# Attention 1 of a graph kernel: the scatter in bfloat16 with three-part messages, the dense sums with the operands exchanged

## The chip, the cores and the metric

The kernel runs on one core of a Trainium2 chip. The metric is the device time of one execution in microseconds (us). A core has five engines with queues of their own, each strictly in order: PE (matrix products), DVE (vector), ACT (scalar functions and copies), POOL (here the issuer of gathers) and SP (the issuer of most DMAs).[...]

## The reference

Two graph layers over 6,250 nodes and 200,000 edges sorted by destination. The first is two graph attentions, the second a convolution with an MLP over edge attributes. The change touches the first attention (4 heads of 16 features):

```python
feat = (x @ W).reshape(num_nodes, H, D)
el = jnp.sum(feat * attn_l[None], axis=-1)
er = jnp.sum(feat * attn_r[None], axis=-1)
e = jax.nn.leaky_relu(el[src] + er[dst], NEG_SLOPE)
m = jax.ops.segment_max(e, dst, num_segments=num_nodes)
ee = jnp.exp(e - m[dst])
s = jax.ops.segment_sum(ee, dst, num_segments=num_nodes)
alpha = ee / s[dst]
msg = feat[src] * alpha[:, :, None]
rst = jax.ops.segment_sum(msg, dst, num_segments=num_nodes)
```

## The kernel before

Nodes are cut into 49 blocks of 128 destinations. Attention 1 treats them in two ways, mixed in one stretch of time.

**Blocks 0 to 30, by edges.** For each block up to 34 chunks of 128 edges are gathered (POOL, L315, one indirect DMA per chunk) in five groups, four of eight chunks and one of two. `attend` (L353) makes for each group a one-hot matrix of destinations on DVE (`one_hot`, L324: `ohr`, four bytes per element), fetches the destination's factors with a matmul per chunk (L360), multiplies them into the gathered features (`msg`, L364 to L370), and splits the message into two parts of the format fp32r, the rounded value by a cast on ACT (L331) and the rest by a subtraction on DVE (L332). Its `scatter` sums with one matmul per chunk: the one-hot is the stationary operand, the two parts side by side (136 columns) are the moving one (L377). When a block is done, ACT copies the first half of the sums and DVE adds the second (L967, L968).

**Blocks 31 to 48, by counts.** For a pair of blocks and each of 7 groups of 7 source blocks, `dense1` (L830) takes a table of how many edges lead from a source node to a destination (`ctc`). For each of four heads ACT makes seven ramps of 128 x 256 (L870), DVE takes the minimum of ramps and counts (`up`, L872, bf16), and PE sums the sources' features over it (L890): the minima of one block are the stationary operand, 102 columns of `rc` (two exponentials x 17 features x three bf16 parts) the moving one, so 14 matmuls for seven source blocks and two destination blocks. Once per group of seven, PE also sums over the plain counts (`every`, L884), here already with the features stationary and 256 columns of counts moving. In `end` (L895) ACT copies `every` to SBUF, PE transposes it, and DVE reduces, subtracts and weighs; the sums of L890 stand with destinations as rows already. `rc` is read from a table `rhs1` in DRAM that `fill_rhs1` (L667) writes in seven steps while blocks 1 and 2 run.

Beside both, `count` (L743) builds the count tables: DVE makes the pair-wise one-hots `lo` and `key` from `slots` (L752, bf16, in PSUM), PE multiplies them (L763), ACT casts the result (L765, `ca`) and issues its DMA to DRAM.

The order is the program's, refined by the scheduler of the tile framework. A hand-written loop gives each group of `attend` a share of counting steps and dense steps. A step's matmuls are put off to the step after it:

```python
    def step(new):

        while late:
            late.popleft()()
        late.extend(new)
```

After attention 1 come attention 2 (all blocks by counts, L1165 to L1170) and the convolution (L1212 on, with `one_hot` and the two-part split of L331 and L332 again).

Of the kernel before, what the change touches and what calls it, by code (L numbers as in the profile page):

```python
# [42 lines left out]
P = 128  # L43
# [23 lines left out]
def gnn_kernel(ctx: ExitStack, tc: tile.TileContext, x, src, dst, attr4, attr8,  # L67
# [207 lines left out]
    srcw = pool.tile([P, NB, K], I32, name="srcw")  # L275
    dstw = pool.tile([P, NB, K], F32, name="dstw")
    raw_dst = {}
# [40 lines left out]

    def one_hot(dl, n, exact=True):
        if exact:  # L320
            oh = work.tile([P, SB, P], F32R, name="ohr", bufs=3)
        else:
            oh = gen.tile([P, GSB, P], F32, name="ohg")
        nc.vector.tensor_tensor(oh[:, :n, :], slot[:, None, :].to_broadcast([P, n, P]),  # L324
                                dl[:, :, None].to_broadcast([P, n, P]), op=OP.is_equal)
        return oh

# [25 lines left out]
    def attend(G, dl, n, oht, pq, H, acc_of, start, stop):  # L353

        oh = one_hot(dl, n)
        pe = ps_pe.tile([P, 512], F32, tag="pe", name="pe")
        for c in range(n):
            nc.tensor.matmul(pe[:, c * 6 * H:(c + 1) * 6 * H], oht[:, c, :], pq, start=True, stop=True)  # L360
        w = aw.tile([P, SB, 2 * H], F32, name=f"w{H}")
        nc.vector.tensor_reduce(w[:, :n, :], pe[:, :n * 6 * H].rearrange("p (c j s) -> p c j s", c=n, s=3),
                                axis=AX.X, op=OP.add)
        nc.vector.tensor_tensor(w[:, :n, :], w[:, :n, :], G[:, :n, HD + H:], op=OP.mult)  # L364
        m = aw.tile([P, SB, HD + H], F32, name=f"msg{H}")
        nc.vector.tensor_tensor(m[:, :n, HD:], w[:, :n, :H], w[:, :n, H:], op=OP.max)
        nc.vector.tensor_tensor(
            m[:, :n, :HD].rearrange("p c (h d) -> p c h d", h=H),
            G[:, :n, :HD].rearrange("p c (h d) -> p c h d", h=H),
            m[:, :n, HD:][:, :, :, None].to_broadcast([P, n, H, HD // H]), op=OP.mult)  # L370
        ms = aw.tile([P, SB, 2, HD + H], F32R, name="halves")
        halve([ms[:, :n, j, :] for j in range(2)], m[:, :n, :])

        def scatter():
            acc = acc_of()
            for c in range(n):
                nc.tensor.matmul(acc, oh[:, c, :], ms[:, c].rearrange("e s f -> e (s f)"),  # L377
                                 start=start and c == 0, stop=stop and c == n - 1)

        return scatter  # L380

    def attend_general(G, dl, n, erc, H, acc, start, stop):


        oh = one_hot(dl, n, False)
        pt = quad()
# [22 lines left out]
    def node_max(G, dl, n, H, most):  # L409

        oh = one_hot(dl, n, False)
        for c in range(n):
# [249 lines left out]
    C1 = 3 * (DH + 1)  # L662
    W1R = 2 * H1 * C1 + 2
    rhs1 = dram.tile([P, NB, W1R], BF16, name="rhs1")
    deg1 = pool.tile([P, DENSE1], F32, name="deg1")

    def fill_rhs1(b0, n):  # L667
        t = dn.tile([P, HS, R1], F32, name="t1c", bufs=1)
        nc.sync.dma_start(t[:, :n], rows_of(table1, b0, n))
        x = dn.tile([P, HS, 2, H1, DH + 1], F32, name="x1", bufs=1)  # L670
        for j in range(2):
            ex = t[:, :n, HD + (1 + j) * H1:HD + (2 + j) * H1]
            nc.vector.tensor_tensor(x[:, :n, j, :, :DH], t[:, :n, :HD].rearrange("p b (h d) -> p b h d", h=H1),
                                    ex[:, :, :, None].to_broadcast([P, n, H1, DH]), op=OP.mult)
            nc.vector.tensor_copy(x[:, :n, j, :, DH:], ex[:, :, :, None])
        r = dn.tile([P, HS, W1R], BF16, name="rc")
        nc.vector.memset(r[:, :, 2 * H1 * C1:], 1.0)
        for j in range(2):
            rj = r[:, :, j * H1 * C1:(j + 1) * H1 * C1].rearrange("p b (f s) -> p b f s", s=3)
            xj = x[:, :n, j].rearrange("p b h d -> p b (h d)")  # L680
            nc.scalar.copy(rj[..., 0], xj)
            nc.vector.tensor_tensor(xj, xj, rj[..., 0], op=OP.subtract)
            nc.scalar.copy(rj[..., 1], xj)
            nc.vector.tensor_tensor(rj[..., 2], xj, rj[..., 1], op=OP.subtract)
        nc.sync.dma_start(rhs1[:, b0:b0 + n], r)
# [144 lines left out]
    def dense1():  # L830
# [14 lines left out]
        for b0 in range(NG, NB, 2):  # L845
# [3 lines left out]
            for h in range(0, H1, 2):  # L849
# [6 lines left out]
                nc.scalar.copy(erb[:, h:h + 2, :n * P], pe.rearrange("p (j c) -> p j c", j=2)[:, :, :n * P])  # L856

            sums = {}
            yield []
            for h0 in range(0, NB, HS):  # L860
                ct, r = ahead
                if h0 + HS < NB:
                    ahead = load(b0, n, h0 + HS)
                by_head = r[:, :, :2 * H1 * C1].rearrange("p b (j h f) -> p b j h f", j=2, h=H1)
                for h in range(H1):
# [9 lines left out]

                    def add(h0=h0, h=h, r=r, ct=ct, up=up, by_head=by_head, b0=b0, n=n, sums=sums):
                        if h0 + h == 0:
                            sums["ups"] = [ps_dn.tile([P, 512], F32, tag=f"up{k}", name=f"up{k}")[:, :2 * H1 * C1].rearrange(
                                "p (h j f) -> p h j f", h=H1, j=2) for k in range(n)]
                            sums["every"] = ps_dn.tile([P, 2, 2 * P], F32, tag="every", name="every")  # L880
                        ups, every = sums["ups"], sums["every"]
                        for i in range(HS if h == 0 else 0):
                            for j in range(2):
                                nc.tensor.matmul(every[:HH + 1, j, :n * P].rearrange("p (k d) -> p k d", d=QN),  # L884
                                                 r[:, i, (2 + j) * HH:(3 + j) * HH + 1],
                                                 ct[:, :n, :, i, :].rearrange("p k a d -> p (k a) d"),
                                                 start=h0 + i + j == 0, stop=h0 + i + j == NB)
                        for i in range(HS):
                            for k in range(n):
                                nc.tensor.matmul(ups[k][:, h], up[:, i, k * P:(k + 1) * P], by_head[:, i, :, h, :],  # L890
                                                 start=h0 + i + h == 0, stop=h0 + i + h == NB + H1 - 2)

                    yield [add]

            def end(b0=b0, n=n, sums=sums):  # L895
# [4 lines left out]
                for k in range(n):  # L900
                    for j in range(2):
                        nc.tensor.transpose(turned[:, k, j, :HH + 1], whole[:, j, k * P:(k + 1) * P],
                                            ident[:HH + 1, :HH + 1])
                s2 = dn.tile([P, 2, H1, DH + 1], F32, name="s2", bufs=1)
                v = dn.tile([P, 2, 2, H1, DH + 1], F32, name="v1", bufs=1)
                for k in range(n):
                    nc.vector.tensor_reduce(s2[:, k].rearrange("p (j h) d -> p j (h d)", j=2),
                                            turned[:, k, :, :HH].rearrange("p j (f s) -> p j f s", s=3),
                                            axis=AX.X, op=OP.add)
                    for j in range(2):  # L910
                        nc.vector.tensor_reduce(v[:, k, j], ups[k][:, :, j].rearrange("p h (d s) -> p h d s", s=3),
                                                axis=AX.X, op=OP.add)
                nc.vector.tensor_copy(deg1[:, b0 - NG:b0 - NG + n, None], turned[:, :n, 1, HH:HH + 1])
                nc.vector.tensor_tensor(v[:, :n, 1], s2[:, :n], v[:, :n, 1], op=OP.subtract)
                for j in range(2):
                    nc.vector.tensor_tensor(v[:, :n, j], v[:, :n, j],
                                            pq[:, b0:b0 + n, j * H1:(j + 1) * H1, None].to_broadcast([P, n, H1, DH + 1]),
                                            op=OP.mult)
                total = fin.tile([P, 2, HD + H1], F32, name="sumsd")
                nc.vector.tensor_add(total[:, :n, :HD].rearrange("p k (h d) -> p k h d", h=H1), v[:, :n, 0, :, :DH],  # L920
                                     v[:, :n, 1, :, :DH])
                nc.vector.tensor_add(total[:, :n, HD:, None], v[:, :n, 0, :, DH:], v[:, :n, 1, :, DH:])
                finish1(b0, n, total[:, :n, :])
# [30 lines left out]
    def attending(b, s, n, oht):  # L954
# [3 lines left out]
        def acc_of():  # L958
            if s == 0:
                kept1["acc"] = whole()[:, :2 * (HD + H1)]  # L960
            return kept1["acc"]

        def end():
            if b % 4 == 0:
                kept1["sums"] = fin.tile([P, 4, HD + H1], F32, name="sums1", bufs=2)
            acc, sums = kept1["acc"], kept1["sums"]
            nc.scalar.copy(sums[:, b % 4, :], acc[:, :HD + H1])  # L967
            nc.vector.tensor_add(sums[:, b % 4, :], sums[:, b % 4, :], acc[:, HD + H1:])  # L968
            if b % 4 == 3 or b == NG - 1:
# [316 lines left out]
    with tc.tile_pool(name="conv", bufs=1) as pool, tc.tile_pool(name="gath3", bufs=6) as gath:  # L1286
# [10 lines left out]
        def hots(t):  # L1297
            n = min(SB, NT - t)
            return one_hot(dstc[:, t:t + n], n)

# [55 lines left out]
        def general3(b, n):  # L1356
            nc.vector.tensor_copy(base, starts[:, ds(b, 1)])
            nc.vector.memset(tot3, 0.0)
            with tc.For_i(0, NCHUNK, 1) as i:
# [11 lines left out]
                for s in range(0, GK, GSB):  # L1371
# [4 lines left out]
                    for c in range(GSB):  # L1376
# [3 lines left out]
                    convolve(G, GSB, at[0][:, cs, 0:1], at[0][:, cs, 1:], a8t,  # L1380
                             lambda c: (acc, s + c == 0, s + c == GK - 1), one_hot(dl[:, cs], GSB))
                for j in range(2):
# [47 lines left out]
```

## Time and profile before

| | |
|---|---|
| median of 3 runs | 4651.73 us (4643.12 to 4654.26) |
| the profiled execution, its span | 4651.0 us, 4649.3 us |
| busy, share of span | DVE 75%, PE 69%, ACT 61%, POOL 60%, PE weight loads 51% |
| granted PE clock, mean | 0.754 |
| moved by DMA | 480.88 MB, 103 GB/s |

Busy shares are means over three stages with different limits, so the stage in question must be read by itself. In the rows of the groups the order is: line, engine, operation, what is written and read, shapes and count; then after the bar the busy time in us, the mean of one in ns; then the engine's idle time just before the group and what ended most of it. Rows of waits give who waited for whom, us in total, how often, and the longest. PE's busy time overlaps itself, because matmuls are pipelined.

### The profile page before, as it was taken

Reading aid. Unit: us, or ns where it says so; the run is one execution under the profiler, and the core shown is the slowest. Engines: PE = TensorE matmul, PEld = TensorE weight load, DVE = VectorE, ACT = ScalarE, POOL = GpSimd, SP = SyncE. Lnnn points to the kernel's source line nnn. Section 1 sums busy time; section 2 is a strip of 40 time slices with the busy share of each in tenths; the row PEclk is TensorE's granted clock in tenths of the full one; section 3 lists DMA queues with packets and bytes.
Section 4 is the critical chain, followed back from the end, with each engine's and each line's share of the span. In section 5 each row is a group of like instructions: output and inputs, shape, how many; then the busy total and the mean of one; then the engine's idle time right before and its main releaser. Section 6 shows DMA issues by size and latency. Waiting matters only on the chain. (4 is left out here: it accounts for less than half of the span.)

```text
span 4649.3 us, 65503 instructions
## 1 busy us (share of the span) xinstructions
PE 3221.1 (69%) x21547; PEld 2384.9 (51%) x21548; DVE 3499.3 (75%) x5685; ACT 2828.8 (61%) x6834; POOL 2785.6 (60%) x2684
## 2 busy tenths in 40 slices
PE   3023676766667766399997678777777777777777
PEld 3013566656566666388885344444444444444444
DVE  4255777878778878488886787788878777878787
ACT  2022578777878888499996554555555555555554
POOL 0677777666566665100002777777777777777774
PEclk9999766666666666599998676677677777766777
DMA  3344455555555555544442222222222222222221
GB/s 86 69 108 125 139 162 145 157 151 156 144 150 163 164 152 149 184 159 157 160 165 73 57 58 59 58 58 58 58 57 59 58 58 58 58 58 58 58 57 32
DMA packets 348162, 480.88 MB, mean 103 GB/s; under 512 B 190737, under 2 KB 236343, under 8 KB 343830
## 3 DMA queue, kind: packets, MB, share of 16 engines
q1 hardware_dynamic: 199542, 240.46, 16.9%
q0 software_dynamic: 85776, 147.31, 13.4%
q10 hardware_dynamic: 62480, 88.68, 5.6%
q8 instruction: 176, 2.88, 0.3%
q14 instruction: 188, 1.54, 0.1%
HBM read 367.21 MB, written 108.97 MB: 102 GB/s over the span
## 5 line engine op out<-in xcount | busy, mean ns | idle before, releaser
L315 POOL DMA_INDIRECT G<-table,srcc x1563 | 1592.8, 1019 | 1027.5 <-DVE kept L1210 551.4
L315 POOL DMA_INDIRECT G<-table,srcw x1054 | 1121.0, 1064 | 568.2 <-issue 279.0
L1262 PE MATMUL whole<-halves,ohr 128*128 128x512 f32 x1563 | 684.8, 596 | 362.2 <-DVE halves L332 320.1
L870 ACT ACTIVATE ramp<-erb,sel 128x256 bf16<-128x256 f32 x1764 | 759.0, 499 | 11.5 <-DVE up L872 8.0
L1262 PEld LDWEIGHTS whole<-halves,ohr 128*128 128x128 f32 x1563 | 427.5, 288 | 607.6 <-DVE halves L332 392.5
L1243 ACT ACTIVATE g<-G,a 128x128 f32<-128x128 f32 x1563 | 511.0, 395 | 43.5 <-DMA G<-table,srcc 35.0
L1161 ACT ACTIVATE ramp<-small,sel 128x256 bf16<-128x256 f32 (+1 forms) x1225 | 447.6, 625 | 61.1 <-DVE up L1165 26.1
L765 ACT CAST ca<-small 128x392 bf16<-128x392 f32 x784 | 342.1, 481 | 192.1 <-PE small L763 180.4
L890 PE MATMUL up<-rc,up 128*128 128x102 bf16 x3528 | 311.4, 264 | 155.9 <-DVE up L872 154.8
L377 PE MATMUL whole<-halves,ohr 128*128 128x136 f32 x1054 | 250.1, 387 | 224.6 <-DVE halves L332 167.7
L763 PE MATMUL small<-key,lo 128*128 128x98 bf16 x3136 | 318.6, 252 | 116.1 <-ACT ca L765 105.3
L1232 PEld LDWEIGHTS big<-wtp_sb,hid 64*128 64x128 f32 x3126 | 256.7, 239 | 204.7 <-ACT hid L1226 100.7
L890 PEld LDWEIGHTS <-up 128*128 128x128 bf16 x3528 | 265.7, 129 | 183.4 <-DVE up L872 177.4
L332 DVE TENSOR_TENSOR halves<-big,halves 128x1024 fp32r<-128x1024 f32 x196 | 237.4, 1211 | 144.3 <-ACT halves L331 144.3
L872 DVE TENSOR_TENSOR up<-ramp,ctc 128x1792 bf16<-128x1792 bf16 x252 | 273.9, 1087 | 92.7 <-ACT ramp L870 71.3
L1224 PE MATMUL small<-hid,wm_sb 128*128 128x512 f32 x392 | 288.0, 825 | 74.4 <-ACT hid L1222 74.2
L377 PEld LDWEIGHTS whole<-halves,ohr 128*128 128x128 f32 x1054 | 217.3, 292 | 237.1 <-DVE halves L332 172.4
L1232 PE MATMUL big<-wtp_sb,hid 64*128 64x128 f32 x3126 | 307.4, 344 | 26.8 <-ACT hid L1226 26.8
L763 PEld LDWEIGHTS <-lo 128*128 128x128 bf16 x3136 | 247.1, 124 | 145.1 <-issue 126.4
L752 DVE TENSOR_TENSOR lo<-slots,turned 128x2048 bf16<-128x2048 bf16 x196 | 239.0, 1219 | 101.4 <-PE small L763 100.2
L1222 ACT ACTIVATE hid<-small 128x512 f32<-128x512 f32 x196 | 116.8, 596 | 313.7 <-PE small L1220 313.7
L331 ACT CAST halves<-mid 128x1024 fp32r<-128x1024 f32 x196 | 204.1, 1041 | 160.9 <-DVE mid L1251 159.2
(292 smaller groups left out, 6196.7 us busy)
## 6 DMA issues: line engine op xcount, KB each, us to landing
counts<-ca ACTq DMA_DIRECT2D x196, 392.0 KB
ct<-counts SPq DMA_DIRECT2D x196, 392.0 KB
rc<-rhs SPq DMA_DIRECT2D x63, 717.5 KB
oht<-dlow SPq DMA_DIRECT2D x31, 1088.0 KB
ctc<-counts SPq DMA_DIRECT2D x504, 56.0 KB
G<-table,srcc POOLq DMA_INDIRECT x1563
G<-table,srcw POOLq DMA_INDIRECT x1054
a8t<-attr_rows SPq DMA_DIRECT2D x391, 16.0 KB
```

Source lines behind the costliest of these rows:

```text
L315: nc.gpsimd.indirect_dma_start(out=G[:, c, :], out_offset=None, in_=table, in_offset=bass.IndirectOffsetOnAxis(ap=idx[:, c:c + 1], axis=0))
L377: nc.tensor.matmul(acc, oh[:, c, :], ms[:, c].rearrange("e s f -> e (s f)"), start=start and c == 0, stop=stop and c == n - 1)
L763: nc.tensor.matmul(ps[:, k * NKEY:(k + 1) * NKEY], lo[:, a, :, r], ky[:, a, :, r], start=True, stop=True)
L765: nc.scalar.copy(ca[:, :, i * W:(i + WBANK) * W].rearrange("p h (k d) -> p h k d", d=W), ps[:, :WBANK * NKEY].rearrange("p (k h d) -> p h ...
L870: nc.scalar.activation(ramp[:, i, :n * P], erb[:, h, :n * P], AF.Relu, bias=sel1[:, h0 + i, h:h + 1], scale=STEEP)
L872: nc.vector.tensor_tensor(up[:, :, :n * P].rearrange("p h (a d) -> p h a d", d=QN), ramp[:, :, :n * P].rearrange("p h (a d) -> p h a d", d ...
L890: nc.tensor.matmul(ups[k][:, h], up[:, i, k * P:(k + 1) * P], by_head[:, i, :, h, :], start=h0 + i + h == 0, stop=h0 + i + h == NB + H1 - 2)
L1161: nc.scalar.activation(ramp[:, h, :n * P], pe[:, :n * P], AF.Relu, bias=sel2[:, h0 + h, :], scale=STEEP)
L1224: nc.tensor.matmul(ph[:, :npr * P], wm2_sb, hid1[:, :npr * P], start=True, stop=True)
L1232: nc.tensor.matmul(pw[:, c, :], hid2[half, j * P:(j + 1) * P], wtp_sb[half].rearrange("x p u -> x (p u)"), start=True, stop=True)
L1243: nc.scalar.activation(g0[:, c], G[:, c, :], AF.Copy, scale=a0[:, c, :])
L1262: nc.tensor.matmul(acc, oh[:, c, :], ms[:, c].rearrange("e s h i u -> e (s h i u)"), start=start, stop=stop)
```

## The change

In `attend`, the one-hot becomes bf16, laid out in pairs of chunks (`pair_hot`, reading `slot_k` as `count` does), for which the destinations `dstw` become bf16 too. The message is split in three bf16 parts (cast, subtract, cast, subtract) instead of two fp32r parts; the moving operand of the scatter is then 204 columns wide, and one reduction over three parts gives the block's sums.

In `dense1`, the operands of the head sums change places: the 102 feature columns of a head are stationary, the minima of both blocks, 256 columns, move, so seven matmuls do what 14 did. The result has features as rows; `end` copies it to SBUF on ACT (`some`), transposes it on PE, four times for each block, and reduces it on DVE. In the table of `rhs1` the columns are ordered by pairs of heads, so that both kinds of sums find their columns side by side; its width stays 410. Some DVE operations in `fill_rhs1` and `end` are cut in two for that order.

```diff
-    dstw = pool.tile([P, NB, K], F32, name="dstw")
+    dstw = pool.tile([P, NB, K], BF16, name="dstw")
...
+    def pair_hot(dl, n):
+
+        oh = aw.tile([P, SB // 2, P, 2], BF16, name="ohp", bufs=3)
+        shape = [P, n // 2, P, 2]
+        nc.vector.tensor_tensor(oh[:, :n // 2], slot_k[:, None].to_broadcast(shape),
+                                dl.rearrange("p (a k) -> p a k", k=2)[:, :, None, :].to_broadcast(shape), op=OP.is_equal)
         return oh
...
-        oh = one_hot(dl, n)
+        oh = pair_hot(dl, n)
...
-        ms = aw.tile([P, SB, 2, HD + H], F32R, name="halves")
-        halve([ms[:, :n, j, :] for j in range(2)], m[:, :n, :])
+
+        ms = aw.tile([P, SB, 3, HD + H], BF16, name="thirds")
+        for j in range(2):
+            nc.scalar.copy(ms[:, :n, j, :], m[:, :n, :])
+            nc.vector.tensor_tensor(ms[:, :n, 2, :] if j else m[:, :n, :], m[:, :n, :], ms[:, :n, j, :], op=OP.subtract)
...
-                nc.tensor.matmul(acc, oh[:, c, :], ms[:, c].rearrange("e s f -> e (s f)"),
+                nc.tensor.matmul(acc, oh[:, c // 2, :, c % 2], ms[:, c].rearrange("e s f -> e (s f)"),
...
+    HW = 4 * C1 + 1
+    W1R = H1 // 2 * HW
...
-                                 r[:, i, (2 + j) * HH:(3 + j) * HH + 1],
+                                 r[:, i, j * HW + C1:j * HW + C1 + HH + 1],
...
+                        q, h = divmod(h, 2)
                         for i in range(HS):
-                            for k in range(n):
-                                nc.tensor.matmul(ups[k][:, h], up[:, i, k * P:(k + 1) * P], by_head[:, i, :, h, :],
-                                                 start=h0 + i + h == 0, stop=h0 + i + h == NB + H1 - 2)
+                            c = q * HW + h * (2 * C1 + 1)
+                            nc.tensor.matmul(ups[q][:2 * C1, h, :n * P], r[:, i, c:c + 2 * C1], up[:, i, :n * P],
+                                             start=h0 + i + h == 0, stop=h0 + i + h == NB)
...
+                some = dn.tile([2 * C1, H1 // 2, 2, 2 * P], F32, name="some", bufs=1)
+                for q in range(H1 // 2):
+                    nc.scalar.copy(some[:, q, :, :n * P], ups[q][:2 * C1, :, :n * P])
...
                 for k in range(n):
+                    turned = bank().rearrange("p (h c) -> p h c", h=H1)
+                    for h in range(H1):
+                        nc.tensor.transpose(turned[:, h, :2 * C1], some[:, h // 2, h % 2, k * P:(k + 1) * P],
+                                            ident[:2 * C1, :2 * C1])
+                    nc.vector.tensor_reduce(v[:, k].rearrange("p q h j d -> p (q h) (j d)"),
+                                            turned[:, :, :2 * C1].rearrange("p h (f s) -> p h f s", s=3),
                                             axis=AX.X, op=OP.add)
...
-                kept1["acc"] = whole()[:, :2 * (HD + H1)]
+                kept1["acc"] = whole()[:, :3 * (HD + H1)]
...
-            nc.scalar.copy(sums[:, b % 4, :], acc[:, :HD + H1])
-            nc.vector.tensor_add(sums[:, b % 4, :], sums[:, b % 4, :], acc[:, HD + H1:])
+            nc.vector.tensor_reduce(sums[:, b % 4, :], acc.rearrange("p (s f) -> p f s", s=3), axis=AX.X, op=OP.add)
...
-            return one_hot(dstc[:, t:t + n], n)
+            return one_hot(dstc[:, t:t + n], n, cw.tile([P, SB, P], F32R, name="ohr", bufs=3))
```

The last line is the convolution's: its one-hot, still fp32r, is taken from a pool that is opened at the start of the convolution and no longer from one that lives through the whole kernel.

More of the change, by code (lines that the diff above doesn't have):

```diff
@@ L317, in gather, with one_hot @@
                 in_offset=bass.IndirectOffsetOnAxis(ap=idx[:, c:c + 1], axis=0))
[L319 to L323, printed above, removed]
+    def one_hot(dl, n, oh):
         nc.vector.tensor_tensor(oh[:, :n, :], slot[:, None, :].to_broadcast([P, n, P]),
                                 dl[:, :, None].to_broadcast([P, n, P]), op=OP.is_equal)
+        return oh
+    def pair_hot(dl, n):
[3 more added lines that the diff above has]
+                                dl.rearrange("p (a k) -> p a k", k=2)[:, :, None, :].to_broadcast(shape), op=OP.is_equal)
         return oh
@@ L382, in attend_general @@
     def attend_general(G, dl, n, erc, H, acc, start, stop):
-        oh = one_hot(dl, n, False)
+        oh = one_hot(dl, n, gen.tile([P, GSB, P], F32, name="ohg"))
         pt = quad()
@@ L409, in node_max @@
     def node_max(G, dl, n, H, most):
-        oh = one_hot(dl, n, False)
+        oh = one_hot(dl, n, gen.tile([P, GSB, P], F32, name="ohg"))
         for c in range(n):
@@ L662, in gnn_kernel @@
     C1 = 3 * (DH + 1)
-    W1R = 2 * H1 * C1 + 2
+    HW = 4 * C1 + 1
+    W1R = H1 // 2 * HW
     rhs1 = dram.tile([P, NB, W1R], BF16, name="rhs1")
@@ L669, in fill_rhs1 @@
         nc.sync.dma_start(t[:, :n], rows_of(table1, b0, n))
-        x = dn.tile([P, HS, 2, H1, DH + 1], F32, name="x1", bufs=1)
+        x = dn.tile([P, HS, H1 // 2, 2, 2, DH + 1], F32, name="x1", bufs=1)
         for j in range(2):
[L672 to L675, printed above, removed]
-        r = dn.tile([P, HS, W1R], BF16, name="rc")
[L677 to L684, printed above, removed]
+            ex = t[:, :n, HD + (1 + j) * H1:HD + (2 + j) * H1].rearrange("p b (q h) -> p b q h", h=2)
+            for h in range(2):
+                xh = x[:, :n, :, h, j if h == 0 else 1 - j]
+                nc.vector.tensor_tensor(
+                    xh[..., :DH], t[:, :n, :HD].rearrange("p b (q h d) -> p b q h d", h=2, d=DH)[:, :, :, h],
+                    ex[:, :, :, h, None].to_broadcast([P, n, H1 // 2, DH]), op=OP.mult)
+                nc.vector.tensor_copy(xh[..., DH:], ex[:, :, :, h, None])
+        r = dn.tile([P, HS, W1R], BF16, name="rc")
+        by_two = r.rearrange("p b (q c) -> p b q c", c=HW)
+        nc.vector.memset(by_two[..., 2 * C1:2 * C1 + 1], 1.0)
+        for h in range(2):
+            rh = by_two[:, :n, :, h * (2 * C1 + 1):h * (2 * C1 + 1) + 2 * C1].rearrange("p b q (f s) -> p b q f s", s=3)
+            xh = x[:, :n, :, h].rearrange("p b q j d -> p b q (j d)")
+            nc.scalar.copy(rh[..., 0], xh)
+            nc.vector.tensor_tensor(xh, xh, rh[..., 0], op=OP.subtract)
+            nc.scalar.copy(rh[..., 1], xh)
+            nc.vector.tensor_tensor(rh[..., 2], xh, rh[..., 1], op=OP.subtract)
         nc.sync.dma_start(rhs1[:, b0:b0 + n], r)
@@ L863, in dense1 @@
                     ahead = load(b0, n, h0 + HS)
-                by_head = r[:, :, :2 * H1 * C1].rearrange("p b (j h f) -> p b j h f", j=2, h=H1)
                 for h in range(H1):
@@ L874, in dense1, with add @@
                                             ct[:, :n].rearrange("p k a h d -> p h (k a) d"), op=OP.min)
-                    def add(h0=h0, h=h, r=r, ct=ct, up=up, by_head=by_head, b0=b0, n=n, sums=sums):
+                    def add(h0=h0, h=h, r=r, ct=ct, up=up, b0=b0, n=n, sums=sums):
                         if h0 + h == 0:
-                            sums["ups"] = [ps_dn.tile([P, 512], F32, tag=f"up{k}", name=f"up{k}")[:, :2 * H1 * C1].rearrange(
-                                "p (h j f) -> p h j f", h=H1, j=2) for k in range(n)]
+                            sums["ups"] = [ps_dn.tile([P, 2, 2 * P], F32, tag=f"up{k}", name=f"up{k}")
+                                           for k in range(H1 // 2)]
                             sums["every"] = ps_dn.tile([P, 2, 2 * P], F32, tag="every", name="every")
@@ L903, in end @@
                                             ident[:HH + 1, :HH + 1])
-                s2 = dn.tile([P, 2, H1, DH + 1], F32, name="s2", bufs=1)
-                v = dn.tile([P, 2, 2, H1, DH + 1], F32, name="v1", bufs=1)
-                for k in range(n):
-                    nc.vector.tensor_reduce(s2[:, k].rearrange("p (j h) d -> p j (h d)", j=2),
-                                            turned[:, k, :, :HH].rearrange("p j (f s) -> p j f s", s=3),
+                some = dn.tile([2 * C1, H1 // 2, 2, 2 * P], F32, name="some", bufs=1)
@@ new lines, in end @@
+                for q in range(H1 // 2):
+                    nc.scalar.copy(some[:, q, :, :n * P], ups[q][:2 * C1, :, :n * P])
+                s2 = dn.tile([P, 2, H1 // 2, 2, DH + 1], F32, name="s2", bufs=1)
+                v = dn.tile([P, 2, H1 // 2, 2, 2, DH + 1], F32, name="v1", bufs=1)
+                for h in range(2):
+                    c = h * (C1 + 1)
+                    nc.vector.tensor_reduce(s2[:, :n, :, h], turned[:, :n, :, c:c + C1].rearrange(
+                        "p k j (f s) -> p k j f s", s=3), axis=AX.X, op=OP.add)
@@ new lines, in end @@
+                nc.vector.tensor_copy(deg1[:, b0 - NG:b0 - NG + n, None], turned[:, :n, 1, C1:C1 + 1])
+                for k in range(n):
+                    turned = bank().rearrange("p (h c) -> p h c", h=H1)
[4 more added lines that the diff above has]
+                                            turned[:, :, :2 * C1].rearrange("p h (f s) -> p h f s", s=3),
@@ L909, in end @@
                                             axis=AX.X, op=OP.add)
+                total = fin.tile([P, 2, HD + H1], F32, name="sumsd")
+                for h in range(2):
+                    vh = [v[:, :n, :, h, j if h == 0 else 1 - j] for j in range(2)]
+                    nc.vector.tensor_tensor(vh[1], s2[:, :n, :, h], vh[1], op=OP.subtract)
                     for j in range(2):
-                        nc.vector.tensor_reduce(v[:, k, j], ups[k][:, :, j].rearrange("p h (d s) -> p h d s", s=3),
-                                                axis=AX.X, op=OP.add)
@@ L913, in end @@
[L913 to L919, printed above, removed]
@@ L920, in end @@
-                nc.vector.tensor_add(total[:, :n, :HD].rearrange("p k (h d) -> p k h d", h=H1), v[:, :n, 0, :, :DH],
-                                     v[:, :n, 1, :, :DH])
-                nc.vector.tensor_add(total[:, :n, HD:, None], v[:, :n, 0, :, DH:], v[:, :n, 1, :, DH:])
+                        f = pq[:, b0:b0 + n, j * H1:(j + 1) * H1].rearrange("p b (q h) -> p b q h", h=2)[:, :, :, h, None]
+                        nc.vector.tensor_tensor(vh[j], vh[j], f.to_broadcast([P, n, H1 // 2, DH + 1]), op=OP.mult)
@@ L923, in end @@
+                    nc.vector.tensor_add(
+                        total[:, :n, :HD].rearrange("p k (q h d) -> p k q h d", h=2, d=DH)[:, :, :, h],
+                        vh[0][..., :DH], vh[1][..., :DH])
+                    nc.vector.tensor_add(total[:, :n, HD:].rearrange("p k (q h) -> p k q h", h=2)[:, :, :, h, None],
+                                         vh[0][..., DH:], vh[1][..., DH:])
                 finish1(b0, n, total[:, :n, :])
@@ L1380, in general3 @@
                     convolve(G, GSB, at[0][:, cs, 0:1], at[0][:, cs, 1:], a8t,
-                             lambda c: (acc, s + c == 0, s + c == GK - 1), one_hot(dl[:, cs], GSB))
+                             lambda c: (acc, s + c == 0, s + c == GK - 1), one_hot(dl[:, cs], GSB, cw.tile([P, SB, P], F32R, name="ohr", bufs=3)))
                 for j in range(2):
```

## The prediction

> **What bounds the kernel now.** The table of the 40 slices, with its clock row, splits the span into three parts: attention 1 to about 1,980 us, attention 2 to about 2,530, the convolution after it. The change lies in the first part, so I cut that by time (the table by stretch; columns are busy time of PE, PE weight loads, DVE, ACT, POOL, then clock, DMA share, GB/s):
>
> ```profile
> 400.00:500.00 100.00, 55.77 (x414) 49.71 (x414) 73.58 (x151) 34.42 (x80) 76.83 (x77) 1.00 0.42 116
> ...
> 700.00:900.00 200.00, 136.77 (x1307) 125.25 (x1305) 155.86 (x263) 162.93 (x405) 136.95 (x125) 0.64 0.54 155
> 1500.00:1700.00 200.00, 141.52 (x1380) 130.23 (x1380) 160.09 (x279) 170.64 (x424) 130.68 (x121) 0.67 0.56 162
> ...
> 1800.00:1900.00 100.00, 69.76 (x720) 64.09 (x717) 78.31 (x116) 89.55 (x220) 24.80 (x22) 0.69 0.45 134
> ...
> 2000.00:2200.00 200.00, 181.83 (x1954) 168.49 (x1955) 174.44 (x310) 185.36 (x508) 0.00 (x0) 1.00 0.45 157
> ```
>
> Up to about 500 us POOL sets the pace: 77 of 100 us busy, the rest of it issue gaps between gathers. From 500 to 1,900 us nobody is full. ACT leads (81 to 85%, and 90% when the gathers are over), DVE follows at 78 to 80%, PE at 68 to 71%. So I read next who waits for whom in 500 to 1,900 us, first PE, then ACT, then DVE:
>
> ```profile
> PE up L890 <- DVE up L872: 153.9, 98, 7.8
> PE small L763 <- ACT ca L765: 97.2, 94, 2.6
> PE every L884 <- DMA rc<-rhs: 94.1, 41, 6.1
> ...
> ACT ca L765 <- PE small L763: 165.4, 115, 6.3
> ACT halves L331 <- DVE msg L367: 34.2, 12, 8.1
> ...
> DVE lo L752 <- PE small L763: 100.2, 84, 6.0
> DVE up L872 <- ACT ramp L870: 66.3, 67, 1.9
> ```
>
> It is a ring of three in-order queues: ACT makes ramps, DVE takes minima of them, PE sums those, and ACT and DVE wait for count matmuls that stand behind the sums in PE's queue. Work added to one link is partly paid by the others. The prices are in the groups by shape, same stretch (count, busy us, mean ns):
>
> ```profile
> L890 PE MATMUL up<-rc,up 128*128 128x102 bf16 x3486 | 307.3, 264 | 155.0 <-DVE up L872 153.9
> L752 DVE TENSOR_TENSOR lo<-slots,turned 128x2048 bf16<-128x2048 bf16 x181 | 220.8, 1220 | 101.4 <-PE small L763 100.2 <-issue 0.4
> L884 PE MATMUL every<-ctc,rc 128*103 128x256 bf16 x882 | 188.7, 378 | 106.8 <-DMA rc<-rhs 94.1 <-DMA counts<-ca 9.3 <-DMA ctc<-counts 3.2
> L752 DVE TENSOR_TENSOR key<-slots,turned 128x1568 bf16<-128x1568 bf16 x181 | 174.5, 964 | 0.0
> L324 DVE TENSOR_TENSOR ohr<-slots,dstw 128x1024 fp32r<-128x1024 bf16 x95 | 115.2, 1213 | 0.0
> L332 DVE TENSOR_TENSOR halves<-msg,halves 128x544 fp32r<-128x544 f32 x96 | 68.6, 715 | 0.3 <-ACT halves L331 0.3
> L331 ACT CAST halves<-msg 128x544 fp32r<-128x544 f32 x96 | 61.9, 645 | 37.8 <-DVE msg L367 34.2 <-DVE inv L512 3.2 <-ACT ca L765 0.4
> ```
>
> **What the Trainium skill says.** "TensorE: Matmul & The Clock Gate", Back-to-back issue gap: N/1.2 ns at the slow clock, N/2.4 + 2.5 at the fast one. The start times in the trace agree: 85 and 46 ns for the 102-column matmuls of L890, 213 and 109 for the 256-column ones of L884, whose 103-column weights thus hide. The fp32 scatter (L377) stands apart: 214 and 112 ns for 136 columns, what 256 columns cost. The same page, Part 1: the clock is either half or full and follows PE's activity. The trace shows both values; records begin at 518 us, so the 1.00 before that means nothing. "VectorE: DVE Perf Modes", The perf-mode tier table, gives any tensor_tensor with a PSUM operand one element per cycle; the trace differs: the two forms of L752 read `slots` in PSUM and differ by 480 elements and 255 ns, 0.53 ns each, two per cycle. L324 needs 1213 ns for half the elements of `lo`.
>
> **The change part by part**, 500 to 1,900 us (96 groups of eight chunks, 24 of two, 252 dense head steps).
>
> *ACT.* A second cast per group. A cast occupies 645 ns, but in the timeline the next instruction starts 0.54 us after it. So 96 x 0.54 + 24 x 0.2 (305 ns less the same overlap) = +57 us. The copy of sums (L967, 204 ns, some 0.1 start to start) goes: -2. Two copies `some` per dense pair, priced as L898's 590 ns less overlap: 18 x 0.5 = +9. Sum **+64 us**.
>
> *DVE.* The one-hot in two-byte pairs: 964 - 544 x 0.53 = 675 ns instead of 1213, so 96 x -0.54 = -52, and 24 small ones at about -0.145 = -3. A second subtraction per group, priced like the one there is (L332, 293 ns for its small form): 96 x 0.715 + 24 x 0.293 = +76. The reduction of `sums` for an addition: 24 x 0.15 = +4. In a pair's end, four reductions of 359 ns become two of 408 elements (575, by L1178's 556 for 390), while adds and products double at 0.2 each: +0.6 us a pair, +5. Sum **+30**, some +20 start to start.
>
> *PE.* Dense sums: 14 matmuls of 102 columns become 7 of 256: 1.19 to 1.49 us at the slow clock, 0.64 to 0.76 at the fast one; 73% of these gaps are slow, so 252 x 0.25 = +63. The scatter has 204 columns and bf16 weights: 170 and 87 ns by the page's formula, 816 x 0.038 = -31. Eight more transposes a pair at L902's 89 to 173 ns: 72 x 0.14 = +10. Sum **+42**, although 1,764 matmuls and as many weight loads go.
>
> *No cost.* The 28 wide groups before 500 us and the rearranged fill of rhs1 (seven times, some 1 us more on DVE) lie beside the gathers, as long as POOL leads there. SP and POOL issue the same DMAs with the same bytes; the row of rhs1 stays 410 wide. The convolution keeps its order on every engine; its one-hots come from a later pool, so the first may start a microsecond or two later.
>
> *The new wait.* The message chain was cast, subtract, scatter; it is now cast, subtract, cast, subtract, scatter. By the built order the second cast stands on ACT behind two count casts and often a ramp and the issue of a counts DMA (about 1.3 us), while DVE reaches the first subtraction behind a `lo` of 1.2 us and takes 0.7. So ACT will stand for some 0.5 us at many of the 120 second casts with the next ramps queued behind it, and PE's scatter waits for the last subtraction with count matmuls behind it. No trace shows this: between 0 and 120 x 1.3 us = 156. A gain by itself I exclude.
>
> *The sum.* ACT leads, and its largest idle group is a wait for PE, which gets work too; I take its 64 in full. Of DVE's 20 and PE's 42 I take a third, 21. Casts that fall into ACT's waits for PE, which are 1.4 us each: -25, an estimate by 120 x 0.54 with four in ten hidden. The new wait: +10, low in its bounds because one third of the second casts has ramps in front. The last pair's end has no cover: +3. Together +73 on 4651.0 us, the profiled execution's own time (span 4649.3), which is 0.7 below the median: **about 4720 us**.
>
> **Rivals.**
> - *PE gets faster, and the kernel with it.* Denser streams could hold the full clock, as attention 2 does (1.00 at PE 91%). If the clock between 500 and 1,900 us rose from 0.66 to 0.85, PE's 950 busy us would shrink by 22%, some 210, and the waits of ACT (165) and DVE (100) for count matmuls by perhaps half, 130. Against the +98 of the terms without the hidden part, that is about -30: 4620. It decides from a clock near 0.8. For it: PE's array work grows while the stage is no longer. Against it: PE would still be starved 154 us by DVE's minima, and more fed work at half clock is not more activity per window by much. Chance 0.15.
> - *Hidden.* ACT's 285 us of idle time in this stretch (1,400 less 1,115 busy) swallow the casts, since a cast can run while count matmuls are awaited: between -10 and +14, 4653. Against it: ACT reaches 90% and no more even without gathers. 0.10.
> - *The round trip dominates.* Second casts wait for DVE at the top of the bounds: +64 + 21 + 156 + 3 less the hidden 25, about +210: 4860. Against it: the built order leaves work between. 0.10.
> - The change does what it says: one-hots, parts and operands are swapped in the built program. The only part that can fail is the paired mode of the one-hot; then DVE keeps 1213 ns, +55 more.
>
> **The numbers.** The forecast case has 0.65, with its own range 4670 to 4780. A measurement of this kernel tells 0.3% (14 us) from no change. Low end 4635 takes in part of the faster case, high end 4800 part of the round trip. Faster: 0.15 and a little of hidden, 0.16. Same: 0.08. Slower: 0.76.
>
> **What would show it.** Right: casts of `thirds` at 645 ns twice per group with ACT at 84 to 88% from 700 to 1,900 us; one-hots near 675 ns; dense matmul starts 213 or 109 ns apart, the scatter's 170 or 87; attention 1 ends some 70 us later and the rest is as long as before. Wrong: a clock over 0.8 in that stretch, or ACT's waits for PE down by more than 60 us with the stage no longer (faster or hidden); waits of ACT casts for DVE above 120 us (round trip); a one-hot still over 1.1 us.

## The result and the profile after

The changed kernel takes 4705.18 us in the median, the kernel before 4647.42 on the same chip: ratio 1.0127, 95% interval 1.0098 to 1.0156, or +58 us. The profiled execution has a span of 4703.5 us, 54 more than before (4649.3). All of it comes from attention 1: its last dense matmul starts at 1,963 us and no longer at 1,908, attention 2 takes 532 us from first to last matmul of L1195 (530 before, L1170), and the convolution 2,082 from first to last matmul of L1287 (2,085 before, L1262).

The stretch from 500 to 1,900 us, first of the kernel before and then of the kernel after, and two shorter stretches of the kernel after (columns as in the prediction's table by stretch):

```profile
500.00:1900.00 1400.00, 954.49 (x9208) 873.08 (x9208) 1090.57 (x1918) 1115.24 (x2760) 897.61 (x830) 0.66 0.53 151
```

```profile
500.00:1900.00 1400.00, 905.81 (x7307) 808.44 (x7306) 1084.18 (x2024) 1132.30 (x2762) 905.89 (x834) 0.71 0.50 147
...
700.00:900.00 200.00, 129.17 (x1029) 115.29 (x1028) 155.56 (x301) 163.71 (x401) 134.86 (x121) 0.70 0.50 146
...
2100.00:2200.00 100.00, 90.97 (x981) 84.08 (x979) 87.10 (x155) 91.27 (x253) 0.00 (x0) 1.00 0.47 162
```

The engines are hardly fuller than before: ACT is busy for 81% of the stretch (80% before), DVE for 77% (78%), PE for 65% (68%), and PE's clock is 0.71 (0.66). The added work of ACT and DVE shows as a longer stage more than as a fuller one. The waits of the kernel after, 500 to 1,950 us, first PE, then ACT, then DVE (the prediction's waits cover 500 to 1,900):

```profile
PE up L905 <- DVE up L886: 134.1, 87, 7.8
PE small L777 <- ACT ca L779: 124.1, 126, 2.6
PE whole L384 <- DVE thirds L379: 81.4, 62, 9.7
...
ACT ca L779 <- PE small L777: 107.1, 82, 6.8
ACT thirds L378 <- DVE msg L379: 88.0, 64, 8.9
...
DVE up L886 <- ACT ramp L884: 105.9, 115, 1.7
DVE lo L766 <- PE small L777: 92.8, 94, 5.2
```

ACT no longer waits 165 us for count matmuls but 107; in exchange its casts wait 88 us for the subtraction (L379). PE's scatter (L384) waits 81 us for the last part, where its predecessor waited 12. DVE waits 106 us for ramps, where it waited 66. The groups by shape of the same stretch:

```profile
L905 PE MATMUL up<-up,rc 128*102 128x256 bf16 x1743 | 339.7, 355 | 138.9 <-DVE up L886 134.1 <-DVE rr L817 3.4 <-issue 0.2
L384 PE MATMUL whole<-thirds,ohp 128*128 128x204 bf16 x822 | 127.3, 308 | 87.8 <-DVE thirds L379 81.4 <-DVE ohp L328 5.7 <-DVE sums L993 0.5
L378 ACT CAST thirds<-msg 128x544 bf16<-128x544 f32 x193 | 124.0, 644 | 105.8 <-DVE msg L379 79.1 <-DVE msg L371 18.3 <-DVE inv L519 3.6
L379 DVE TENSOR_TENSOR msg<-msg,thirds 128x544 f32<-128x544 f32 x97 | 69.6, 718 | 1.6 <-ACT thirds L378 1.5
L328 DVE TENSOR_TENSOR ohp<-slots,dstw 128x1024 bf16<-128x1024 bf16 x96 | 65.3, 681 | 0.0
L921 ACT COPY some<-up 102x512 f32<-102x512 f32 x16 | 9.1, 593 | 1.2 <-PE up L905 1.2
```

The prices of single instructions were as predicted: casts 644 ns, subtractions 718, one-hots 681, copies of `some` 593. The new wait is seen in the timeline of ACT and then of DVE, a stretch after 1,404 us (start, length, engine, what; idle time before it in brackets):

```profile
1404.64 0.65 ACT L378 CAST thirds<-msg 128x544 bf16<-128x544 f32 x1
1405.19 0.86 ACT L779 CAST ca<-small 128x392 bf16<-128x392 f32 x2
1405.95 0.52 ACT L884 ACTIVATE ramp<-erb,sel 128x256 bf16<-128x256 f32 x1
...
1407.07 0.65 ACT L378 CAST thirds<-msg 128x544 bf16<-128x544 f32 x1 [0.60 <-DVE msg L379]
```

```profile
1405.18 1.23 DVE L766 TENSOR_TENSOR lo<-slots,turned 128x2048 bf16<-128x2048 bf16 x1
1406.32 0.71 DVE L379 TENSOR_TENSOR msg<-msg,thirds 128x544 f32<-128x544 f32 x1
1406.95 0.97 DVE L766 TENSOR_TENSOR key<-slots,turned 128x1568 bf16<-128x1568 bf16 x1
1407.84 0.72 DVE L379 TENSOR_TENSOR thirds<-msg,thirds 128x544 bf16<-128x544 f32 x1
```

The first cast is done at 1405.3. DVE has `lo` in front of the subtraction and ends the subtraction at 1407.0. ACT, after two count casts and a ramp, stands 0.6 us. Over the stage about half of the second casts waited, 64 of some 120, and for longer than here: 1.4 us on average (88.0 us in all) and 8.9 at most.

### The profile page after: what moved, and what is told of

The parts are those of the page before. It is cut to its first block, busy times and chain, and to the rows that moved or that the text cites. A ratio compares the mean times of both kernels' runs of the same rounds, so it can differ in the third digit from the quotient of the medians.

```text
span 4703.5 us, 62487 instructions
## 1 busy us (share of the span) xinstructions
PE 3188.6 (68%) x19855; PEld 2325.3 (49%) x19856; DVE 3529.5 (75%) x5895; ACT 2911.2 (62%) x6976; POOL 2790.2 (59%) x2684
## 5 line engine op out<-in xcount | busy, mean ns | idle before, releaser
L1287 PE MATMUL whole<-halves,ohr 128*128 128x512 f32 x1563 | 683.2, 594 | 363.5 <-DVE halves L336 321.3
L1287 PEld LDWEIGHTS whole<-halves,ohr 128*128 128x128 f32 x1563 | 427.0, 287 | 607.6 <-DVE halves L336 393.0
L905 PE MATMUL up<-up,rc 128*102 128x256 bf16 x1764 | 344.4, 355 | 140.1 <-DVE up L886 135.3
L777 PE MATMUL small<-key,lo 128*128 128x98 bf16 x3136 | 303.1, 246 | 142.8 <-ACT ca L779 133.7
L378 ACT CAST thirds<-msg 128x544 bf16<-128x544 f32 (+1 forms) x310 | 177.8, 577 | 345.7 <-DVE msg L379 224.3
L905 PEld LDWEIGHTS <-rc 128*102 128x102 bf16 x1764 | 285.0, 170 | 154.9 <-issue 146.5
L384 PE MATMUL whole<-thirds,ohp 128*128 128x204 bf16 x1054 | 172.0, 321 | 276.9 <-DVE thirds L379 268.1
```

Of the source, the lines that this page charges most:

```text
L777: nc.tensor.matmul(ps[:, k * NKEY:(k + 1) * NKEY], lo[:, a, :, r], ky[:, a, :, r], start=True, stop=True)
L905: nc.tensor.matmul(ups[q][:2 * C1, h, :n * P], r[:, i, c:c + 2 * C1], up[:, i, :n * P], start=h0 + i + h == 0, stop=h0 + i + h == NB)
L1287: nc.tensor.matmul(acc, oh[:, c, :], ms[:, c].rearrange("e s h i u -> e (s h i u)"), start=start, stop=stop)
```

## The experiments

Theory A: the message chain (second cast, second subtraction, and the waits between them) carries the loss, the exchanged dense sums are about even. Theory B: the exchanged sums carry it. Theory C: neither alone, only both together.

**Each part alone, first attempt.** The edits are taken from the change itself: e1 has `pair_hot`, `thirds` and what reads them, e2 has `rhs1`, the seven matmuls and the new `end`. e3 drops the third part (the block's sums are then of two parts) and e4 moves the second cast to DVE:

```diff
 e3    ms = aw.tile([P, SB, 2, HD + H], BF16, name="thirds")
       nc.scalar.copy(ms[:, :n, 0, :], m[:, :n, :])
       nc.vector.tensor_tensor(ms[:, :n, 1, :], m[:, :n, :], ms[:, :n, 0, :], op=OP.subtract)
 e4 -  nc.scalar.copy(ms[:, :n, j, :], m[:, :n, :])
    +  (nc.vector.tensor_copy if j else nc.scalar.copy)(ms[:, :n, j, :], m[:, :n, :])
```

> The kernel before with the scatter's part of the change alone (bf16 one-hots in pairs, three message parts); the dense sums are as before. Theory A (the message chain's second cast and subtraction carry the loss): at least as slow as the whole change, 4700 to 4725 us, ACT's waits for DVE in the casts near 110 us as in the whole change. Theory B (the loss comes from the exchanged dense sums, whose PE columns grow, and from their longer end): the scatter alone within 15 us of 4647.

> The kernel before with the dense sums' part alone; the scatter keeps fp32r and two parts. Theory A: 4630 to 4655 us, PE clock between 500 and 1,900 us up from 0.66, ACT's waits for count matmuls below 165 us. Theory B: 4690 us or more.

> The changed kernel with two bf16 parts of the message instead of three: second cast and second subtraction are left out, and with them the message's last eight bits. Theory A: the loss is gone and the cheaper one-hot is left as a gain, 4600 to 4640 us. Theory B: what it saves on ACT was not on the path, 4690 us or more.

> The changed kernel with the second cast of a message on DVE instead of ACT. Theory A in its form 'ACT's load and the round trip to DVE': ACT loses 57 us and two crossings of engines, DVE gains about 120 casts of some 0.4 us, 50 us: 4680 to 4700 us, ACT's waits for DVE in the casts back near 40 us. A form of it in which only total work in the ring of engines counts: 4700 to 4715, no change. If DVE is the tighter engine: 4720 or more.

The kernel before took 5574.9 us in the runs beside these four, not 4647, and they took 5571 to 5607. Ratios: e1 0.998 (0.9954 to 1.0007), e2 1.0003 (0.998 to 1.0025), e3 1.0049 (1.0031 to 1.0068), e4 0.9982 (0.9961 to 1.0003). In e1 ACT's largest wait, from 500 to 2,300 us, is put down to `remote`, which is none of the core's engines, 76 times and up to 23 us:

```profile
ACT ca L772 <- remote: 325.1, 76, 23.3
```

Such stretches stop DVE, PE and POOL as well and also occur in the convolution, which the change leaves alone. What they are stays open. Differences of one per cent in a stage that is stopped for hundreds of us say nothing of the stage itself, so I draw nothing from these four. The kernels that follow had 4645 to 4652 us of the kernel before beside them, e11 and e12 on the same chip as these four. Each ratio is to the kernel before beside it. Each trace is of one execution, and those of e5, e6 and e7 are of executions 7 to 9 us slower than their medians, so their waits are good for their kind and not to the last us.

**Each part alone, again.** e5 is the kernel of e1, e6 that of e2.

> The scatter's part of the change alone, a second time: on the chip of the first four kernels the kernel before took 5575 us instead of 4647, with all engines standing still together again and again, so that those ratios say little of an undisturbed run. Theory A (message chain): ratio 1.010 to 1.018 to the kernel before. Theory B (exchanged dense sums): 0.997 to 1.003. The disturbed chip's ratio of 0.998, if it holds, is against A.

> The dense sums' part alone, a second time, for the same reason. Theory A: ratio 0.996 to 1.002. Theory B: 1.009 or more. If neither part loses 0.5% alone, the loss is in their meeting (theory C: each part's added ACT work fits into ACT's waits, both together don't).

e5, the scatter: 1.0056 (1.0039 to 1.0073), +26 us. e6, the dense sums: 1.0021 (1.001 to 1.0032), +10 us. B falls in its strong form. A gets the larger share, though not all: e5 lies below A's band of 1.010 to 1.018, and the two together give 0.77%, under the whole's 1.27%, whose interval begins at 0.98%. With the intervals of the parts the gap is 0.5%, give or take 0.35%, barely outside chance; if it is real, some part of the loss comes from their meeting (C in a weak form). ACT's two largest waits and PE's for the last part in e5:

```profile
ACT ca L772 <- PE small L770: 95.4, 83, 4.9
ACT thirds L378 <- DVE msg L379: 95.1, 64, 9.5
```

```profile
PE whole L384 <- DVE thirds L379: 92.2, 64, 10.5
```

In e6 (500 to 1,950 us) the exchanged matmuls are as costly as in the whole change, but ACT's wait for count matmuls, 169 us, is about the 165 of before:

```profile
L898 PE MATMUL up<-up,rc 128*102 128x256 bf16 x1764 | 353.6, 362 | 157.1 <-DVE up L879 156.0
...
ACT ca L772 <- PE small L770: 169.1, 117, 7.5
```

So the trace shows no delay of the counts by the sums' longer stream.

**The third part taken away.** e7 is e3 again, e8 the same with the dense sums of before.

> The changed kernel with two bf16 parts of the message instead of three, a second time (the first stood on the disturbed chip); the message loses its last eight bits. It takes away the second cast (57 us of ACT) and the second subtraction (some 65 us of DVE) and keeps the cheaper one-hot. If the message chain carries the loss: ratio 0.990 to 1.001 to the kernel before. If the exchanged dense sums or the bf16 scatter itself carry it: 1.008 or more.

> Two bf16 parts and one-hots in pairs, dense sums as before: the message loses its last eight bits as well. One cast and one subtraction as in the kernel before, the one-hot 55 us of DVE cheaper, scatter matmuls shorter. Theory A: faster than before, ratio 0.982 to 0.996. If DVE's time is worth nothing because ACT sets the pace: 0.997 to 1.003.

e7: 1.0003 (0.9996 to 1.0011). e8: 0.9962 (0.995 to 0.9975), 18 us faster than before. e7 lies in the band of the message chain; e8, at 0.9962, ends just above theory A's band. So the third part costs 1.0056 less 0.9962, 0.94% or 44 us, with the old dense sums, and 1.24% with the new ones. The paired bf16 one-hot and the bf16 scatter together gain 0.38%. Which of the two gains it isn't parted: the one-hot takes some 55 us off DVE, and the scatter's matmuls start about half as far apart as before. In e8's waits the scatter's is down to 32 us and no cast waits for a subtraction:

```profile
PE whole L383 <- DVE thirds L378: 32.4, 23, 8.6
...
ACT ca L771 <- PE small L769: 144.7, 108, 6.3
ACT thirds L377 <- DVE msg L371: 48.3, 16, 6.9
```

e8 beats both kernels, for a price: its messages keep two bf16 parts and lose the third.

**The load without the chain, in the kernel before.** One more cast, or one more subtraction, per group into a tile that nobody reads:

```diff
+        more = aw.tile([P, SB, HD + H], BF16, name="more")
 e9  +   nc.scalar.copy(more[:, :n, :], ms[:, :n, 0, :])
 e10 +   nc.vector.tensor_tensor(more[:, :n, :], m[:, :n, :], ms[:, :n, 0, :], op=OP.subtract)
```

> The kernel before with one more cast per group on ACT, whose result nobody reads: ACT's 57 us without the round trip to DVE. If the load on ACT is what costs: ratio 1.005 to 1.010 (most of what the scatter's part alone lost, 1.0056). If the round trip through DVE costs: 1.000 to 1.003.

> The kernel before with one more subtraction per group on DVE, whose result nobody reads: 69 us and some more of DVE, no new wait between engines. If the ring of queues shares its load, the same as for ACT: ratio 1.004 to 1.010. If ACT alone sets the pace: 0.998 to 1.003.

e9: 1.0033 (1.0019 to 1.0047), 15 us. e10: 1.0024 (1.0014 to 1.0034), 11 us. e9 lies between its two bands; e10 lies in the band of "ACT alone sets the pace", though its interval lies wholly above no change. The groups of e9 and then of e10 show that the load is what it was meant to be:

```profile
L374 ACT CAST more<-halves 128x544 bf16<-128x544 f32 x96 | 62.3, 649 | 1.1 <-issue 0.4
```

```profile
L374 DVE TENSOR_TENSOR more<-msg,halves 128x544 bf16<-128x544 f32 x97 | 69.8, 720 | 0.0
```

So 57 us of ACT (96 x 0.54 + 24 x 0.2) became 15, 0.27 us per us; 77 us of DVE (with 7.4 for the small ones) became 11, 0.14. The two are counted differently, ACT's from start to start and DVE's as busy time: by busy time ACT's 70 us give 0.22. The intervals reach from 9 to 22 us and from 7 to 16, so the runs don't say that ACT's work is the dearer. They do say that either kernel is slower, by much less than the length of what was added. Where some of the rest went is in the waits of e9, 500 to 1,950 us: ACT waits 146 us for count matmuls, 19 less than before, while DVE now waits 102 us for ramps, 36 more. (DVE waits 111 us for ramps in e8 too, which adds nothing to ACT, so that wait alone isn't a measure of ACT's load.)

```profile
ACT ca L767 <- PE small L765: 146.3, 105, 8.3
...
DVE up L874 <- ACT ramp L872: 102.1, 98, 3.3
```

One rival is left. The scheduler of the tile framework orders the whole program anew for each of these kernels, so the load isn't the only thing that differs. Up to the last dense matmul DVE has 2,540 other instructions in e9; 2,205 of them stand in the order of the kernel before, and in e10 2,113. On ACT it is 2,856 and 2,905 of 2,986. Two executions of one kernel (e1 and e5) differ in one of 2,694 on DVE. What the changed order costs or gains was not measured, here or for the parts of the change.

**Chain or load.** e11 is e5 with e4's edit. e12 is e8 with the added instructions of e9 and e10.

> The scatter's part alone (1.0056) with the second cast of a message on DVE: the chain cast, subtract, cast, subtract crosses engines once instead of three times; ACT loses 57 us, DVE gains some 120 x 0.4 us. If the crossings cost (ACT's 95 us of waits for the first subtraction, PE's 92 us for the last): ratio 1.000 to 1.003. If the added work costs wherever it stands: by the measured 0.27 us per us on ACT and 0.16 on DVE, 15 off and 8 on, 1.003 to 1.005, and PE's wait for the last subtraction stays above 70 us.

> Two parts in pairs with the dense sums as before (0.9962), plus one more cast on ACT and one more subtraction on DVE per group whose results nobody reads: the third part's load without its chain and without its 68 columns; the message loses its last eight bits. If load alone explains the third part (0.9962 to 1.0056): 1.004 to 1.006. If the loads add as they did in the kernel before (0.0033 and 0.0024): 1.001 to 1.003, and the rest, some 15 us, belongs to the chain and the wider scatter.

e12: 1.003 (1.0018 to 1.0042), in the band in which the loads add as they did in e9 and e10. Against e8 the load costs 0.68%, of the 0.94% that the third part costs. The remaining 0.26% (12 us, give or take 10) is left for the chain, the 68 further columns and the changed order, which the runs don't part; the intervals of e12 and e5 overlap.

e11: 1.0044 (1.0031 to 1.0058), in the band of "the added work costs wherever it stands"; it is 0.12% under e5, inside both intervals: undecided whether faster. Its waits, PE's, then ACT's:

```profile
PE small L770 <- ACT ca L772: 103.2, 114, 2.6
PE whole L384 <- DVE thirds L379: 87.4, 62, 8.0
...
ACT ca L772 <- PE small L770: 156.3, 116, 5.0
```

The casts' 95 us of waits for DVE (e5) are gone, and ACT waits 156 us for count matmuls instead of 95. ACT's idle time from 500 to 1,900 us did not fall with the round trip: it is 301 us in e11 and 261 in e5, for ACT has one cast less per group. So the time that ACT stood behind the round trip was, as far as these two traces show, time that it would have stood elsewhere. PE's wait for the last part is 87 us, hardly less than the 92 of e5.

## Why the prediction was right, and where its terms were not

*Direction and size.* Forecast 4720 us, +73 by its sum (which is 4724); measured 4705, +58. The likeliest case happened: more work for ACT and DVE made attention 1 longer and the rest stayed as long as before, with PE at 213 and 109 ns per dense matmul and 169 and 87 per scatter matmul. ACT at 84 to 88% from 700 to 1,900 us did not come: it has 83% there, after 82% before. The shares read from before (ACT 81 to 85%, DVE 78 to 80, PE 68 to 71) fit only part of the 500 to 1,900 us: from 500 to 700 they are 68, 73 and 65%, and ACT's mean is 80. The clock records of before begin at 508 us and not at 518.

*ACT "in full", mis-sized.* The sum took ACT's 64 us whole, less 25 for hidden casts. e9 priced 57 us of such work at 15, so some 42 were hidden. ACT's busy share led, but much of what was added stands where ACT had waited for count matmuls (165 us before, 107 in the whole change).

*DVE, a third of a net sum.* The fraction was 0.14 by e10, not a third. Netting the cheaper one-hot against the second subtraction, and the shorter scatter against the longer dense sums, hid that the paired one-hot and the bf16 scatter are a gain of their own: e8 is 18 us faster than before.

*PE, mis-sized.* +73 us of array time for the dense exchange, a third of it on the path, with ACT's and the end's share, would be some 36 us for this part by the sum's own rule (24 + 9 + 3). e6 measured 10, with an interval of 5 to 15. One reason shows in the trace of e6: 63% of the gaps between dense matmuls are slow ones, where 73% were before, and the mean gap is 171 ns for 74. So 252 steps cost about 42 us more array time (7 matmuls for 14) and not 63, and by the same rule the part comes to 29. The rest of the difference is not explained. The prediction gave little chance to the faster clock as a cause of a gain in the whole, rightly, but the clock did move, from 0.66 to 0.71, a quarter of the way to the 0.85 that this rival assumed.

*The new wait, right in place and cause.* 88 us of waits lie within 0 to 156. The half microsecond at many second casts was 1.4 us on average at about half of them. Its cost (10 taken) is compatible with the 12 us, give or take 10, that e12 leaves for chain, columns and order together.

*What made the total fit.* In part it was luck. The sum over-priced the added work, but the two parts measured alone give 26 and 10 us, 36 of the 58, and the remaining 22 us (give or take 16) stand in no term of the sum. The same shows in the third part, which cost more beside the new sums than beside the old (1.24% and 0.94%, with intervals of some 0.3 and 0.2% either way that overlap). Whether there is an interaction, and whether it lies in the ring or in the order that the scheduler chose, stays open.

The rivals: the round trip did not dominate (4705 us, not 4860; its own terms add up to 219 us and not 210), hidden fell (+58), and the faster PE did not carry the kernel.

## What to carry to other kernels

In this ring of in-order queues, with its two fullest engines near 80%, added work cost a fraction of its length on each, 0.27 us per us on ACT and 0.14 on DVE. Such fractions can be measured by adding work to one engine whose result nobody reads; one should then also look whether the scheduler kept the order of the rest. A format that makes a step cheaper and another that makes it longer should be priced apart: the paired bf16 one-hot with the bf16 scatter was worth keeping, the third part cost more than twice their gain. A wait that appears in a trace isn't a cost until the waits that it replaces are counted.

## What the runs showed of the hardware

The granted PE clock, from 500 to 1,900 us, was 0.66 in the kernel before, 0.70 with the exchanged sums alone (e6) and 0.71 in the changed kernel. The mean over the whole span was 0.766 to 0.777 in all 22 executions of e6 and 0.753 to 0.761 in the 27 of the kernel before beside them. PE's busy time (954 us before, 964 in e6, 906 after) doesn't tell the work apart from the clock, for the same matmul of 256 columns starts 213 ns after the one before at the slow clock and 109 at the fast one. The exchange isn't all that moves the clock: with the old sums it was 0.66 in e5, 0.68 in e8 and e12 and 0.69 in e11. Why it rose stays open.

The matmuls of the fp32r scatter with 136 columns started 112 or 214 ns apart (at the faster and the slower clock), whereas 136 columns in bf16 (e8) start 59 or 113 ns apart and 204 columns (after) 87 or 169. So the number of columns did not set the former pace; the format of the operands did, or the paired layout of the one-hot, which changed with it.

A DVE cast of 544 elements from SBUF to bf16 took 440 ns (e11) where ACT takes 643.
